# A graph layer's own rows: four transfers instead of one, sums of shares in PSUM, and a strip added in five parts

## The chip, the core and the metric

The kernel runs on one core of a Trainium2 chip. The metric is the device time of one execution in microseconds, taken as the median of several runs. The core has a matrix engine (TensorE: PE, with its weight loads as PEld), a vector engine (VectorE: DVE), a scalar engine (ScalarE: ACT), GpSimd (POOL) and an engine for synchronisation (SyncE: SP). Here POOL issues the gathers of rows and SP issues nearly all other transfers.

## The reference

One layer of a graph network over 50,000 nodes with 160 features and 1,650,000 edges, which are sorted by destination. 800,000 random pairs give an edge in each direction, and every node has an edge to itself.

```python
s, v = x[:, :64], x[:, 64:].reshape(n, 32, 3)
ss, vv = s[src], v[src]
e0, e1 = sh[:, 0:1], sh[:, 1:4]              # edge_attr_4
dot = einsum('eui,ei->eu', vv, e1)
out0 = C0 * (ss * e0 @ W1 + dot * INV3 @ W2)
p3 = (ss @ W3)[:, :, None] * e1[:, None, :] * INV3
p4 = einsum('eui,uw->ewi', vv * e0[:, :, None], W4) * INV3
p5 = einsum('eui,uw->ewi', cross(vv, e1[:, None, :]), W5) * INV6
m = concat([out0, (C1 * (p3 + p4 + p5)).reshape(-1, 96)])
m_agg = segment_sum(m, dst)
h = concat([m_agg[:, :64] @ Ws * LIN_S, (vector part of m_agg) @ Wv * LIN_V])
return layernorm(x + x + relu(h))
```

All of it up to the relu is linear in the source's row and in the edge's four attributes. So for every node it is enough to have four weighted sums of source rows, one for each attribute k: the sum over its edges of attr[e, k] * x[src[e]]. One product with a combined weight matrix then gives h.

## The kernel before

**Gathers and group sums.** Edges are taken in groups of 6 x 128, two groups to a "pair", 1044 pairs in all. For each pair POOL issues 12 indirect gathers, each of 128 rows of x, into a tile `xg` (line 349; four such tiles exist). DVE builds `hot` (line 358: which of a window of 32 nodes an edge belongs to; one input, `slotsP`, lies in PSUM) and `ha` (line 361: hot times the four attributes `pk`, which lie in PSUM). PE multiplies ha with the gathered rows (line 386), so that PSUM holds, for 4 attributes x 32 nodes, the sums over the group. DVE transposes them in blocks of 32 (line 398) and adds them at the right columns of a ring buffer (line 405, columns from a register).

**The ring.** `ring[k]` holds the sums of segment k, which is 512 nodes (S = 512), as 128 partitions (4 attributes x 32 features) x 5 blocks of features x TW = 768 nodes. Since sums of a segment's last groups run past its end, the first 256 columns of the next segment get what stands beyond column 512 of the one before (line 402, one addition over 5 x 256 columns, both inputs in SBUF).

**Own rows.** After the first 100 groups, edges that lead from a node to itself are no longer gathered. A "pack" step (16 packs, lines 463 to 628) takes them out of the edge lists: it compacts the other edges into `edges` in DRAM, sums each node's attributes of its own edges, and stores these "shares", four numbers a node, in `selves` in DRAM. Then for each two blocks of 128 nodes, `ask_own` (lines 661 to 684) loads their 256 rows of x into `xr`, once for each of the four attributes, which are four quarters of 32 partitions: partition 32k + w holds 8 nodes for attribute k. The load is one transfer whose source has a leading dimension of four copies with step 0 (line 675). A second transfer (line 676) loads into `sr` the one share that belongs to each partition and node. `set_own` (lines 686 to 696) multiplies xr by sr on DVE (line 689, both inputs in SBUF) and transposes the result into the ring (line 693), where later sums are added to it.

**Nodes.** For each block of 128 nodes PE multiplies the ring's five blocks with the weights (line 704), DVE adds x and takes mean and variance (lines 182 to 186), ACT takes the root (line 191), DVE scales (lines 195, 196), and SP stores two blocks at once (line 784). `ahead` loads x for this (line 644).

**Order.** The order is written by hand. `after_pair(p, f, ...)` hands f over when the program has written out pair p; `work(1.0)` then takes tasks from a queue, one credit for each gather's matmul. For a segment that begins at pair p (10 to 12 pairs after the one before), `begin_segment` is handed over at p - 3, ask_own at p - 6 and set_own at p - 2. Packs have due times (line 834), the earlier of one that follows from when the packed edges are loaded and one that follows from the first segment that needs their shares. Every engine runs its instructions in the order written; SP's queue holds the loads, the stores of packs (line 618) and the stores of results in one order.

**PSUM.** `bank` (line 243) is one bank of 4 x 128 numbers a partition. Its first quarter is `slotsP`; the second and third take transposes of indices (lines 326, 327); columns 0 to 19 of the fourth take the first node of each group (line 320).

Of the kernel before, what the change touches and what calls it, by code (L numbers as in the profile page):

```python
# [39 lines left out]
F32 = mybir.dt.float32  # L40
# [4 lines left out]
ALU = mybir.AluOpType  # L45
AX = mybir.AxisListType
# [4 lines left out]
P = 128  # L51
MUL0, MUL1 = 64, 32
D = MUL0 + 3 * MUL1
NK = 4
# [9 lines left out]
W = 32  # L64
QG = P // W
FB = P // NK
ND = D // FB
PG = 2
# [3 lines left out]
BP = 2  # L72
# [30 lines left out]
def tile_gnn_resnorm(ctx: ExitStack, tc: tile.TileContext, x, src, dst, attr, W1, W2, W3, W4, W5, Ws, Wv, out, n_edges):  # L103
    nc = tc.nc
# [97 lines left out]
    def near(g):  # L202
        p = g * G * P
        return p / degree if p <= EH else EH / degree + (p - EH) / (degree - 1)

    nblocks = math.ceil(N / P)
    S = SB * P
# [11 lines left out]
    high = [min(math.ceil(near(g)) + off_of[g // SG] + 1, N - 1) for g in range(NG)]  # L219
# [3 lines left out]
    TW = max(h - k * S for h, k in zip(high, seg_of)) + W  # L223
    first_of = [seg_of.index(k) for k in range(NSEG)]
    last_of = [max(g for g in range(NG) if low[g] < (b + 1) * P) for b in range(nblocks)]

    with tc.tile_pool(name="once", bufs=1) as once, tc.tile_pool(name="raw", bufs=2) as rawp, \
# [8 lines left out]
        spotp, ownp = (later_pools.enter_context(tc.tile_pool(name=name, bufs=bufs))  # L236
                       for name, bufs in (("spot", 3), ("own", 2)))
# [5 lines left out]
        bank = psC.tile([P, 4, P], F32, name="bank")  # L243
        slotsP = bank[:, 0, :]
        nc.vector.tensor_copy(slotsP, slots)

        dq = nc.sync
        begun = []
# [27 lines left out]
        spot_of, spots_of, ring = {}, {}, {}  # L276
# [117 lines left out]
        def turn_sums(p, ps):  # L394

            s, g, ng = pairs[p]
            at = sump.tile([P, PG, ND, W], F32, name="sums")
            nc.vector.transpose(at[:, :ng], ps[:, :ng].rearrange("p g (b f) -> p g b f", f=FB))  # L398
            for i in range(ng):
                k = seg_of[g + i]  # L400
                if k and g + i == first_of[k]:
                    nc.vector.tensor_tensor(ring[k][:, :, :TW - S], ring[k][:, :, :TW - S], ring[k - 1][:, :, S:],  # L402
                                            op=ALU.add)
                here = ring[k][:, :, ds(find(g + i), W)]
                nc.vector.tensor_tensor(here, here, at[:, i], op=ALU.add)  # L405

# [6 lines left out]
        def row_start(r):  # L413

            lo, hi = (math.floor(r * L * (1 - 1 / degree)) - 2 * FAR - 2, math.ceil(r * L * (1 - 1 / degree)) + 2 * FAR + 2)
            return (max(lo, 0), hi if r else 0), (max(math.floor((EH + r * L) / degree) - FAR - 2, 0),
                                                  math.ceil((EH + r * L) / degree) + FAR + 2)

        edges = dram.tile([1, (row_start(NR - 1)[0][1] + L) * C], F32, name="edges")
        selves = dram.tile([1, (row_start(NR - 1)[1][1] + W) * NK], F32, name="selves")  # L420
# [209 lines left out]
        def rows_of(b):  # L630
            nb = min(P, N - b * P)
            return nb, slice(b * P, b * P + nb)
# [25 lines left out]
                return []  # L658
            return [list(range(b, min(b + BP, nblocks))) for b in range(k * SB, min((k + 1) * SB, nblocks), BP)]

        def ask_own(k, bs, got):

            n0, n1 = rows_of(bs[0])[1].start, rows_of(bs[-1])[1].stop
            assert rows_stored[0] == NR or row_start(rows_stored[0])[1][0] >= n1
            n = n1 - n0
            nq = next(q for q in range(math.ceil(n / W), n + 1) if n % q == 0)
            m = n // nq
            assert nq <= BP * P // W
            xr = ownp.tile([P, BP * P // W, D], F32, name="xr")
            sr = ownp.tile([P, BP * P // W], F32, name="sr")  # L670
            xs = x[n0:n1, :].rearrange("(w q) d -> w (q d)", q=nq).unsqueeze(0).to_broadcast([NK, m, nq * D])
            ss = selves[0, n0 * NK:n1 * NK].rearrange("(w q k) -> k w q", q=nq, k=NK)
            with nc.allow_non_contiguous_dma(reason="one number of each node"):
                if m == W:
                    dq.dma_start(xr[:, :nq].rearrange("p q d -> p (q d)"), xs)
                    dq.dma_start(sr[:, :nq], ss)
                else:
                    nc.vector.memset(xr[:, :nq], 0.0)
                    nc.vector.memset(sr[:, :nq], 0.0)
                    for k_ in range(NK):  # L680
                        r = slice(k_ * W, k_ * W + m)
                        dq.dma_start(xr[r, :nq].rearrange("p q d -> p (q d)"), xs[k_])
                        dq.dma_start(sr[r, :nq], ss[k_])
            got.extend((xr, sr, nq))

        def set_own(k, bs, got):

            xr, sr, nq = got
            nc.vector.tensor_tensor(xr[:, :nq], xr[:, :nq], sr[:, :nq].unsqueeze(2).to_broadcast([P, nq, D]), op=ALU.mult)  # L689
            c0 = bs[0] * P - k * S  # L690
            c1 = (bs[-1] + 1) * P - k * S
            assert c0 + nq * W <= TW
            nc.vector.transpose(ring[k][:, :, c0:c0 + nq * W].rearrange("p b (w q) -> p q b w", q=nq),  # L693
                                xr[:, :nq].rearrange("p q (b f) -> p q b f", f=FB))
            if c0 + nq * W < c1:
                nc.vector.memset(ring[k][:, :, c0 + nq * W:c1], 0.0)
# [28 lines left out]
        spots = once.tile([1, 2 * npacks * RP], I32, name="spots")  # L725
        limit = once.tile([P, 1], F32, name="limit")
        nc.vector.memset(limit, float(KM))
        none = once.tile([P, 1], I32, name="none")
        nc.vector.memset(none, 0)
        packed = once.tile([P, 2, 2 * npacks], F32, name="packed")  # L730
# [10 lines left out]
        def after_pair(p, f, *args):  # L741
            later.setdefault(p, []).append((f, args))
# [83 lines left out]
        per = SG // PG  # L826

        packs, due = [], []
        for i in range(npacks):

            first = next(s for s in range(NH // SG, NSC)
                         if min(NG, (s + 1) * SG) * G * P - EH > row_start(i * RP)[0][0])
            own = next((k for k in range(NSEG) if min((k + 1) * S, N) > row_start(i * RP)[1][0] and own_blocks(k)), NSEG - 1)
            due.append(min((first - 1) * per - 1, first_of[own] // PG - 7))
            packs.append(pack(i))
        done, began = 0, START

# [1 line left out]
        for k in range(1, NSEG):  # L839
            p = first_of[k] // PG  # L840
            after_pair(max(p - 3, START), begin_segment, k)
            for bs in own_blocks(k):
                got = []
                after_pair(p - 6, ask_own, k, bs, got)
                after_pair(p - 2, set_own, k, bs, got)
        for b, g in enumerate(last_of):
            p = g // PG
# [5 lines left out]
        for p, (s, g, ng) in enumerate(pairs):  # L853
# [34 lines left out]
            if p == START - 1:  # L888
                with ExitStack() as behind, tc.tile_pool(name="table", bufs=1) as tablep:
                    for i in first_ones:  # L890
# [3 lines left out]
                               allow_small_or_imprecise_dtypes=True)  # L894
# [13 lines left out]
    base = const.tile([P, NB], F32, name="base")  # L908
# [6 lines left out]
    with tc.tile_pool(name="up", bufs=1) as up, tc.tile_pool(name="us", bufs=2) as us, tc.For_i(0, once_more, 1):  # L915
# [12 lines left out]
                       allow_small_or_imprecise_dtypes=True)  # L928
        nc.gpsimd.iota(hib, pattern=[[NBLK, CB]], base=NBLK, channel_multiplier=NBLK * CB,
                       allow_small_or_imprecise_dtypes=True)  # L930
        nseg = NU // SEG
        far = up.tile([PB, 2, CB, nseg], F32, name="far2")
        for s in range(nseg):
# [4 lines left out]
                           allow_small_or_imprecise_dtypes=True)  # L938
            nc.gpsimd.iota(num[:, 1], pattern=[[1, SEG]], base=s * SEG + 1, channel_multiplier=0,
                           allow_small_or_imprecise_dtypes=True)  # L940
# [10 lines left out]
        f = up.tile([PB, CB], F32, name="f")  # L951
# [104 lines left out]
```

## Time and profile before

| What | us |
|---|---|
| Median of 3 runs | 17993.09 (17978.58 to 18013.7) |
| Profiled execution, its own time | 18022.17 |
| Profiled execution, span | 18020.0 |
| Stream transpose of own rows, line 693, x188 | 466.1 busy, 2479 ns each |
| Group sums into PSUM, line 386, x25044 | 6255.4 busy on PE |
| Move of group sums, line 398, x1044 | 529.7 busy, 507 ns each; 6341.5 idle before them |
| Clearing of a ring, line 653, 128x1280, x93 | 104.6 busy, 1125 ns each |
| Granted TensorE clock, mean | 0.625 |

The profile is of one execution. "Busy" counts the time in which an engine executed, "idle before" the time that its engine stood before an instruction of the group, with what ended it; "issue" there is time in which the engine waited for nothing that the profile shows, and "remote" a release that the profile couldn't place. SPq marks issues on SP's queue. The mean of a group can hide a long tail, which the minimum, median and maximum of a line show. In 40 equal slices of the span every engine's share is nearly the same from start to end, so one stretch can stand for the others.

### The profile page before, as it was taken

The page shows a single profiled execution, that of the slowest core. Times are in us where ns is not written, and L with a number is a line of the kernel's source. Part 1 is how long each engine was busy: PE and PEld are TensorE (multiplying, and loading weights), DVE is VectorE, ACT ScalarE, POOL GpSimd, SP SyncE. Part 2 cuts the span into 40 slices and gives each one's busy share as a digit, 9 for nine tenths or more (in the row PEclk, how much of TensorE's full clock was granted, in tenths as well). Part 3 has the DMA queues.
Part 4 walks back from the last instruction along what each step waited for, and adds up shares of the span by engine and source line. Part 5 has one row for each costly group of instructions (what it writes and reads, how often), then busy time and mean ns, then how long its engine had stood idle before and what let it go on. Part 6 is the DMA issues. An engine that isn't in the chain of part 4 may idle for free. (4 is left out here: it accounts for less than half of the span.)

```text
span 18020.0 us, 99721 instructions
## 1 busy us (share of the span) xinstructions
PE 6879.0 (38%) x29811; PEld 6014.7 (33%) x29812; DVE 7032.6 (39%) x11269; ACT 227.8 (1%) x479; POOL 12137.8 (67%) x12535
## 2 busy tenths in 40 slices
PE   3333334343333333333333333334333333333333
PEld 3333333333333333333333333333333333333333
DVE  4343443434434343443433434344343433434332
ACT  0000000000000000000000000000000000000000
POOL 6666666666666666666666666666666666666666
PEclk6666666666666666666666666666666666666666
DMA  2222323232232322323223232322323223232222
GB/s 71 74 69 72 80 71 81 69 82 72 73 79 70 83 71 73 79 69 81 72 72 79 70 79 72 82 69 72 80 70 82 69 73 80 69 79 72 73 72 63
DMA packets 961715, 1337.18 MB, mean 74 GB/s; under 512 B 411739, under 2 KB 716048, under 8 KB 957182
## 3 DMA queue, kind: packets, MB, share of 16 engines
q0 software_dynamic: 601056, 1026.60, 23.7%
q1 hardware_dynamic: 358674, 302.87, 6.1%
q8 instruction: 238, 3.90, 0.1%
q14 instruction: 307, 2.51, 0.0%
q10 hardware_dynamic: 1440, 1.29, 0.0%
HBM read 1258.50 MB, written 71.40 MB: 74 GB/s over the span
## 5 line engine op out<-in xcount | busy, mean ns | idle before, releaser
L349 POOL DMA_INDIRECT xg<-in_x,si x12522 | 12134.1, 969 | 5859.5 <-issue 3666.1
L386 PE MATMUL ps<-xg,ha 128*128 128x160 f32 x25044 | 6255.4, 383 | 9081.8 <-issue 8146.9
L386 PEld LDWEIGHTS ps<-xg,ha 128*128 128x128 f32 x25044 | 5171.1, 254 | 9859.0 <-issue 8902.6
L398 DVE STREAM_TRANSPOSE sums<-ps 128x320 f32<-128x320 f32 x1044 | 529.7, 507 | 6341.5 <-remote 4050.5
L361 DVE TENSOR_TENSOR ha<-hot,pk 128x1536 f32<-128x1536 f32 x1044 | 1830.2, 1753 | 35.8
L182 DVE SCALAR_TENSOR_TENSOR y<-phb,xt 128x160 f32<-128x160 f32 x391 | 125.6, 321 | 3508.3 <-PE ps L386 1623.2
L704 PE MATMUL phb<-BWk,ring 128*128 128x160 f32 (+1 forms) x3910 | 1181.7, 388 | 454.0 <-issue 452.9
L704 PEld LDWEIGHTS phb<-BWk,ring 128*128 128x128 f32 (+1 forms) x3910 | 925.6, 266 | 470.0 <-issue 469.5
L405 DVE TENSOR_TENSOR ring<-ring,sums 128x160 f32 x2087 | 683.1, 327 | 309.7 <-issue 224.2
L358 DVE TENSOR_TENSOR hot<-bank,rel 128x384 f32<-128x384 f32 x1044 | 572.4, 548 | 107.0 <-remote 70.5
L693 DVE STREAM_TRANSPOSE ring<-xr 128x1280 f32<-128x1280 f32 x188 | 466.1, 2479 | 6.5
L566 DVE COPY_PREDICATED prow<-marks,prow 128x2370 f32<-128x2370 int32 (+8 forms) x160 | 445.4, 2784 | 1.1
L320 PE MATMUL bank<-first,ones 120*128 120x20 f32 (+1 forms) x210 | 59.4, 365 | 815.1 <-DVE first L318 573.0
L320 PEld LDWEIGHTS bank<-first,ones 120*128 120x128 f32 (+1 forms) x210 | 49.8, 292 | 853.6 <-DVE first L318 597.5
L191 ACT ACTIVATE rstd<-mv,eps_t 128x1 f32<-128x1 f32 x391 | 115.2, 295 | 17061.4 <-DVE st L184 5415.1
L326 PE MATMUL bank<-ident,r 120*128 120x120 f32 x100 | 46.2, 462 | 703.1 <-issue 361.0
L566 DVE COPY_PREDICATED pra<-marks,pra 128x1580 f32<-128x1580 int32 (+8 forms) x160 | 306.5, 1915 | 0.0
L689 DVE TENSOR_TENSOR xr<-xr,sr 128x1280 f32<-128x1280 f32 x188 | 277.0, 1473 | 57.4 <-DMA sr<-selves 35.9
L326 PEld LDWEIGHTS bank<-ident,r 120*128 120x128 f32 x100 | 21.1, 211 | 727.4 <-issue 369.7
L196 DVE TENSOR_SCALAR o<-y,mv,rstd 128x160 f32<-128x160 f32 x391 | 146.1, 374 | 19.6 <-issue 3.7
L402 DVE TENSOR_TENSOR ring<-ring 128x1280 f32<-128x1280 f32 x97 | 143.0, 1474 | 1.8
L331 PE MATMUL pk<-ident,r 120*128 120x120 f32 (+1 forms) x400 | 139.5, 400 | 0.0
(349 smaller groups left out, 2156.2 us busy)
## 6 DMA issues: line engine op xcount, KB each, us to landing
xg<-in_x,si POOLq DMA_INDIRECT x12522
xr<-in_x SPq DMA_DIRECT2D x187, 640.0 KB
edges<-prow SPq DMA_DIRECT2D x1994, 18.5 KB
r<-edges SPq DMA_DIRECT2D x99, 360.0 KB
selves<-mine SPq DMA_DIRECT2D x1992, 0.5 KB
xt<-in_x SPq DMA_DIRECT2D x195, 160.0 KB
out<-o SPq DMA_DIRECT2D x195, 160.0 KB
pra<-in_attr SPq DMA_DIRECT2D x15, 1580.0 KB
```

The costliest lines, as they stand in the source:

```text
L196: nc.vector.tensor_scalar(o[:n], y[:n], mv[:n, 0:1], rstd[:n], op0=ALU.subtract, op1=ALU.mult)
L349: nc.gpsimd.indirect_dma_start(out=xg[:, j, :], out_offset=None, in_=x, in_offset=bass.IndirectOffsetOnAxis(ap=placed[0][:, u + j:u + j + ...
L358: nc.vector.tensor_tensor(hot[:, :n], slotsP[:, 0:W].unsqueeze(1).to_broadcast([P, n, W]), rel[:, u:u + n].unsqueeze(2).to_broadcast([P, n ...
L361: nc.vector.tensor_tensor(ha[:, :n], hot[:, :n].unsqueeze(2).to_broadcast([P, n, NK, W]), pk[:, :, u:u + n].rearrange("p k u -> p u k").un ...
L386: mm = nc.tensor.matmul(ps[:, j // G, :], ha[:, j].rearrange("p k w -> p (k w)"), xr, start=j % G == 0, stop=j % G == G - 1)
L398: nc.vector.transpose(at[:, :ng], ps[:, :ng].rearrange("p g (b f) -> p g b f", f=FB))
L402: nc.vector.tensor_tensor(ring[k][:, :, :TW - S], ring[k][:, :, :TW - S], ring[k - 1][:, :, S:], op=ALU.add)
L405: nc.vector.tensor_tensor(here, here, at[:, i], op=ALU.add)
L566: nc.vector.copy_predicated(what[:n, a:e], mi[:, r].unsqueeze(2).to_broadcast([n, e - a, what.shape[2]]), what[:n, a + d:e + d])
L689: nc.vector.tensor_tensor(xr[:, :nq], xr[:, :nq], sr[:, :nq].unsqueeze(2).to_broadcast([P, nq, D]), op=ALU.mult)
L693: nc.vector.transpose(ring[k][:, :, c0:c0 + nq * W].rearrange("p b (w q) -> p q b w", q=nq), xr[:, :nq].rearrange("p q (b f) -> p q b f", ...
L704: wrote("misc", nc.tensor.matmul(ph[:nb], ring[k][:, i, c0:c0 + nb], BWk[:, i, :], start=i == 0, stop=i == ND - 1))
```

## The change

Four things change. The rows of x for own edges are loaded by four transfers of 32 partitions each, handed over at p - 8, p - 7, p - 6 and p - 5, in place of one of 128 partitions at p - 6. The shares are loaded as they lie in DRAM, all four of each node to every partition (`sa`, 8 nodes x 4 shares), together with the first part. set_own multiplies sa by a constant mask `shareP` (1 where the partition's quarter is k), sums over k into `sumP`, and multiplies xr by sumP; shareP and sumP lie in PSUM, in unused columns of `bank`. Last, the strip that passes from one ring to the next is added in five operations, one for each block of features, and only over `past` columns, as far as sums of the segment before can reach. The packs' due time by the segment's need is two pairs earlier, in step with the earlier first part.

```diff
+        shareP, sumP = bank[:, 3, 64:64 + NK], bank[:, 3, 96:96 + BP * P // W]
...
-                    nc.vector.tensor_tensor(ring[k][:, :, :TW - S], ring[k][:, :, :TW - S], ring[k - 1][:, :, S:],
-                                            op=ALU.add)
+                    past = max(high[first_of[k - 1]:first_of[k]]) + W - k * S
+                    for b in range(ND):
+                        nc.vector.tensor_tensor(ring[k][:, b, :past], ring[k][:, b, :past], ring[k - 1][:, b, S:S + past],
+                                                op=ALU.add)
...
-        def ask_own(k, bs, got):
+        def ask_own(k, bs, got, part):
...
-            xs = x[n0:n1, :].rearrange("(w q) d -> w (q d)", q=nq).unsqueeze(0).to_broadcast([NK, m, nq * D])
-            ss = selves[0, n0 * NK:n1 * NK].rearrange("(w q k) -> k w q", q=nq, k=NK)
...
-                    dq.dma_start(xr[:, :nq].rearrange("p q d -> p (q d)"), xs)
-                    dq.dma_start(sr[:, :nq], ss)
...
+            if part == 0:
+                xr = ownp.tile([P, BP * P // W, D], F32, name="xr")
+                sa = ownp.tile([P, BP * P // W, NK], F32, name="sa")
...
+            r = slice(part * W, part * W + m)
+            dq.dma_start(xr[r, :nq].rearrange("p q d -> p (q d)"), x[n0:n1, :].rearrange("(w q) d -> w (q d)", q=nq))
+            shares = selves[0, n0 * NK:n1 * NK].rearrange("(w f) -> w f", w=m)
+            if m < W:
+                dq.dma_start(sa[r, :nq].rearrange("p q k -> p (q k)"), shares)
+            elif part == 0:
+                dq.dma_start(sa[:, :nq].rearrange("p q k -> p (q k)"),
+                                shares.unsqueeze(0).to_broadcast([NK, W, nq * NK]))
...
-            nc.vector.tensor_tensor(xr[:, :nq], xr[:, :nq], sr[:, :nq].unsqueeze(2).to_broadcast([P, nq, D]), op=ALU.mult)
+            nc.vector.tensor_tensor(sa[:, :nq], sa[:, :nq], shareP.unsqueeze(1).to_broadcast([P, nq, NK]), op=ALU.mult)
+            nc.vector.tensor_reduce(sumP[:, :nq], sa[:, :nq], axis=AX.X, op=ALU.add)
+            nc.vector.tensor_tensor(xr[:, :nq], xr[:, :nq], sumP[:, :nq].unsqueeze(2).to_broadcast([P, nq, D]), op=ALU.mult)
...
+        quarter = once.tile([P, NK], F32, name="quarter")
+        of_k = once.tile([P, NK], F32, name="of_k")
+        nc.gpsimd.iota(quarter, pattern=[[-W, NK]], base=0, channel_multiplier=1, allow_small_or_imprecise_dtypes=True)
+        nc.vector.tensor_scalar(of_k, quarter, 0.0, None, op0=ALU.is_ge)
+        nc.vector.scalar_tensor_tensor(shareP, quarter, float(W), of_k, op0=ALU.is_lt, op1=ALU.mult)
...
-            due.append(min((first - 1) * per - 1, first_of[own] // PG - 7))
+            due.append(min((first - 1) * per - 1, first_of[own] // PG - 9))
...
-                after_pair(p - 6, ask_own, k, bs, got)
+                for part in range(NK):
+                    after_pair(p - 8 + part, ask_own, k, bs, got, part)
```

## The prediction

> **What bounds the kernel now.** I read the engine sums and the costliest groups first, then POOL's waits, then timelines and a table by stretch. The groups (line, engine, operation, tile; busy us, mean ns of one; idle time before them and what ended it):
>
> ```profile
> PE 6879.0 (38%) x29811; PEld 6014.7 (33%) x29812; DVE 7032.6 (39%) x11269; ACT 227.8 (1%) x479; POOL 12137.8 (67%) x12535
> ...
> L349 POOL DMA_INDIRECT xg<-in_x,si x12522 | 12134.1, 969 | 5859.5 <-issue 3666.1
> ...
> L361 DVE TENSOR_TENSOR ha<-hot,pk 128x1536 f32<-128x1536 f32 x1044 | 1830.2, 1753 | 35.8
> ...
> L405 DVE TENSOR_TENSOR ring<-ring,sums 128x160 f32 x2087 | 683.1, 327 | 309.7 <-issue 224.2
> ...
> L689 DVE TENSOR_TENSOR xr<-xr,sr 128x1280 f32<-128x1280 f32 x188 | 277.0, 1473 | 57.4 <-DMA sr<-selves 35.9
> ...
> L402 DVE TENSOR_TENSOR ring<-ring 128x1280 f32<-128x1280 f32 x97 | 143.0, 1474 | 1.8
> ```
>
> POOL does nothing but 12,522 gathers. The answer on line 349 gives their median as 949 ns. POOL's waits (total us, times, longest):
>
> ```profile
> POOL xg L349 <- issue: 3666.1, 11991, 2.1
> POOL xg L349 <- PE ps L386: 1224.7, 236, 46.9
> POOL xg L349 <- remote: 875.2, 223, 7.0
> ```
>
> Between gathers that wait for nothing lie 3666.1/11991 = 0.306 us. So the span divides: 12,522 x (0.949 + 0.306) = 15,715 us of floor; 12,134.1 - 12,522 x 0.949 = 251 us by which gathers are longer than the median; and pauses of 1224.7 + 875.2 + some 93 in smaller rows = 2193, of which 531 x 0.306 = 162 is floor already, leaving 2031. With 30 us before the first and after the last gather that is 18,027 against a span of 18,020.
>
> The pauses come about like this (timeline; start, us, engine, line; in brackets idle time before):
>
> ```profile
> 2999.47 0.42 PE L704 MATMUL phb<-BWk,ring 128*128 128x160 f32 x1 [2.38 <-issue]
> ...
> 3002.27 0.43 PE L386 MATMUL ps<-xg,ha 128*128 128x160 f32 x1 [2.38 <-issue]
> ...
> 3005.77 6.51 PE L386 MATMUL ps<-xg,ha 128*128 128x160 f32 x32
> ...
> 3006.24 0.95 POOL L349 DMA_INDIRECT xg<-in_x,si  x1 [6.21 <-PE phb L704]
> ```
>
> While POOL gathers without a break, PE slows to one instruction in 0.70 or 1.40 us, though its rows have long been there; the four tiles of xg fill, POOL stands 6.21 us, and PE at once runs 32 matmuls in 6.51 us. SP shows the same 0.70 us steps. These pauses return every 24 or 36 gathers from start to end. So POOL is the bound, but with a tax on every gather.
>
> **What the long gathers cost.** Here two of them stand beside the product:
>
> ```profile
> 1415.84 0.95 POOL L349 DMA_INDIRECT xg<-in_x,si  x1 [0.30 <-issue]
> 1415.89 1.48 DVE L689 TENSOR_TENSOR xr<-xr,sr 128x1280 f32<-128x1280 f32 x1
> ...
> 1417.09 1.09 POOL L349 DMA_INDIRECT xg<-in_x,si  x1 [0.31 <-issue]
> ...
> 1419.74 2.32 POOL L349 DMA_INDIRECT xg<-in_x,si  x1 [0.30 <-issue]
> 1419.76 1.48 DVE L689 TENSOR_TENSOR xr<-xr,sr 128x1280 f32<-128x1280 f32 x1
> ```
>
> The gather that starts with the second product takes 2.32 us. I laid all gathers of the timeline beside the DVE lines they overlap and summed what they took over 949 ns (counting those over 970): beside L689, 186 gathers and 184 us; beside L402, 96 gathers and 51 us, part of which belongs to the L405 right behind it. Beside L361, whose second input is in PSUM, it is 6 us over 2196 gathers. L689 and L402 read both inputs from SBUF.
>
> Do these microseconds count? The stretches (length, POOL busy and its gathers, granted clock, DMA):
>
> ```profile
> 146.00:745.00 599.00, 400.40 (x420) 0.62 0.25 64
> 3191.00:3790.00 599.00, 405.98 (x421) 0.62 0.29 71
> 14633.00:15231.00 598.00, 409.97 (x421) 0.63 0.32 80
> ```
>
> The first lies before the first L689 (840.7 us). The later ones carry 5.6 and 9.6 us more POOL time for the same gathers and take no longer: pauses shrink as the gathers stretch. To put a number on it I cut the gather stream into pieces of 48, left out those with a pause over 7 us, and fitted length against the excess in it: 0.23 (+-0.14) us per us. Pieces of 24 to 180 gave 0.16 to 0.51. I take 0.3; ends 0 and 1.
>
> **The change, part by part.**
>
> *Product from PSUM.* sumP takes the place of sr, so the product has L361's operands: one in SBUF, one in PSUM. L361 costs 1753 ns for 1536 elements and L358 548 for 384, 1.046 ns an element, so 1280 take 1.49 us against 1.473: nothing on DVE. The 184 us of excess go. Times 0.3: -55 us (0 to -184).
>
> *Two small operations before it.* Nearest rows: L358 scaled to 32 elements, 548 - 352 x 1.046 = 180 ns, and the reduction at L341 (278 ns for 120 elements), some 190 ns. 188 x 0.37 = 70 us of DVE, none with two SBUF inputs. The three set-up operations cost under 1 us, once.
>
> *Strip in five parts.* `past` from the plan's numbers is 133 to 256 columns, mean 215 (256 before). Between L405 (160: 327 ns) and L402 (1280: 1474) lies 1.024 ns an element, so a piece is 383 ns and five are 1.91 us against 1.47: 97 x 0.44 = +43 us of DVE. L405 is the row for a piece: outside L402's surroundings it lengthens gathers by some 29 us over 2087, 14 ns each, so 485 pieces give 7 us against 51. Times 0.3: -13 us (0 to -44; +0 if a piece blocks like a fifth of the whole).
>
> These +113 us of DVE I cost at nothing: DVE is busy 39%, and its group sums<-ps idles 6341.5 us waiting for PE. With no cover at all they are +113. What a late set_own holds up is hot and ha (L358, L361) queued behind it on DVE, then PE.
>
> *Four transfers, one of shares.* SP's queue (issues, with the time SP was held):
>
> ```profile
> 1232.34 0.57 SPq L675 DMA_DIRECT2D xr<-in_x  x1
> ...
> 1233.54 12.48 SPq L675 DMA_DIRECT2D xr<-in_x  x1
> ```
>
> Two issues per pair of blocks become five: 187 x 3 = 561 more, at L676's median 0.53 us, 297 us of SP; at the 1.40 of the slow spells 785. Removed are spells like the 12.48, one in each of 93 segments if parts no longer fill the queue: up to 93 x 11.9 = 1107 us. SP waits 4767.2 us for DVE's o at L784, which covers either. Costed 0; ends below. The first part is asked at p-8 and needs the buffer that set_own of the segment before (10 to 12 pairs earlier, at p-2) frees: free by then, and the sends queued behind it wait for later DVE work. Only the first pack's due time moves (38 to 36; the others are set by the edges' term).
>
> The Trainium skill speaks against four transfers: "DMA: Bandwidth & Descriptors", Rules for kernel authors, says two transfers to disjoint partition parts serialize and one over 128 partitions is better. The same table says that an outermost dimension of four copies keeps a transfer to four engines, which is how xr is asked today and fits the 12.48 us hold. By the first rule the loads would last longer, by the second shorter; neither moves the sum while the loads come early.
>
> They do: from the issue of sr to its product pass 99 us or more in three quarters of the cases.
>
> *Sum.* -55 - 13 = -68 on 18,020: 17,952. The profiled run's 18,022 stands 29 us above the median of three, 17,993.09, so -68 there gives **17,925 us**. I count under 0.2% (36 us) as no change.
>
> **Rivals.**
> *B, every microsecond counts* (pass-through 1): -228, 17,765. For: POOL is the bound. Against: the three stretches.
> *C, all absorbed, or the product still blocks*: 17,990. For: the first stretch has hardly any excess and is no faster; PE's slow spells set the rhythm. Against: fits of 0.16 to 0.51, none at 0; L361's 6 us.
> *D, slower: the fourth part lands late at pack ends.* It is asked at p-5, one pair (18,020/1044 = 17.3 us) later than xr today. Where SP is busy storing a pack, sr is issued only 12 to 55 us before the product (24 of 187 cases, some 12 pack ends). With 17 us less, DVE would stand there, ha behind it, PE behind that. The cover is the rows waiting in xg; beyond it POOL pauses. At about 10 us for each of 12 to 16 pack ends it is +120 to +160: 18,130 us. It decides where the lead today is under 17 us plus landing. Against: the 12.5 us hold that eats that lead goes; DVE has waited for sr just 53.6 us in all, 7 times. The extra DVE work without cover (+113) ends at the same place.
>
> **How the numbers follow.** A (partial) 0.52, B 0.12, C 0.16, D 0.20. A's own range is 17,875 to 17,960 by pass-throughs 0.51 to 0.16; 0.06 of it lies within 0.2%. Faster: 0.46 + 0.12 = 0.58; same: 0.06 + 0.16 = 0.22; slower: 0.20. The range cuts off about half of B and half of D: 17,800 to 18,080.
>
> **What would show it.** After: mean gather near 951 ns (POOL busy some 11,910); no long gather beside the product; L402's successor with 485 pieces near 383 ns; the product near 1.48 us; SP's holds on x gone. If pauses (PE ps + remote, 2100 us) rise by 160 or so, A holds; if they stay, B; by 228, C. A wait of DVE on xr or sa in the hundreds of us, or POOL pauses over 10 us at more pack ends than today, shows D. I am wrong if the pauses change for a reason of their own: they are 2031 us, nine times what is removed, and a tenth of them outweighs the sum.

## The result, and the profile after

Twenty runs of each kernel on one chip: 17,992.66 us before, 18,020.46 us after (17,999.86 to 18,037.71), ratio 1.0015, 95% interval 1.0008 to 1.0022. The change lost 0.15%, inside the 0.2% that I count as no change, where 0.4% was to be gained. The profiled execution's span is 18,025.6 us, against 18,020.0.

The groups of the changed kernel (line, engine, operation, tile; busy us, mean ns of one; idle time before them), with the engine sums ahead:

```profile
PE 7001.9 (39%) x29811; PEld 6106.9 (34%) x29812; DVE 7105.0 (39%) x12035; ACT 228.4 (1%) x479; POOL 11879.9 (66%) x12536
...
L350 POOL DMA_INDIRECT xg<-in_x,si x12522 | 11876.1, 948 | 6114.2 <-issue 3647.6
...
L694 DVE TENSOR_TENSOR xr<-xr,bank 128x1280 f32<-128x1280 f32 x188 | 278.8, 1483 | 61.7 <-DMA xr<-in_x 53.8
...
L405 DVE TENSOR_TENSOR ring<-ring 128x196 f32<-128x196 f32 (+20 forms) x485 | 149.0, 372 | 1.8
```

POOL's busy time fell from 12,137.8 to 11,879.9 us, by 258 us, and a gather's mean from 969 to 948 ns. That is all the prediction wanted from the gathers. The product takes 1483 ns and a piece of the strip 372. Two products in the timeline, with the gathers beside them:

```profile
2715.15 0.95 POOL L350 DMA_INDIRECT xg<-in_x,si  x1 [0.30 <-issue]
...
2715.63 1.49 DVE L694 TENSOR_TENSOR xr<-xr,bank 128x1280 f32<-128x1280 f32 x1
...
2716.41 0.95 POOL L350 DMA_INDIRECT xg<-in_x,si  x1 [0.32 <-issue]
...
2719.93 1.49 DVE L694 TENSOR_TENSOR xr<-xr,bank 128x1280 f32<-128x1280 f32 x1
2720.16 0.95 POOL L350 DMA_INDIRECT xg<-in_x,si  x1 [0.30 <-issue]
```

No gather is stretched here: the three that overlap a product take 0.95 us, where one took 2.32 before. Over all 188 products the gathers beside them are longer by 0.2 us in total, where it was 184. But the span did not shrink, and POOL's waits say where the time went (us in total, times, longest):

```profile
POOL xg L350 <- issue: 3647.6, 11959, 1.1
POOL xg L350 <- PE ps L387: 1449.7, 251, 35.3
POOL xg L350 <- remote: 901.4, 226, 6.8
```

The waits for PE and the unplaced ones went from 1224.7 + 875.2 = 2099.9 to 1449.7 + 901.4 = 2351.1 us, up 251. The gathers gave 258 us and POOL's pauses took 251. The three stretches that the prediction looked at (length, POOL busy and its gathers, granted clock, DMA share, GB/s) agree:

```profile
146.00:745.00 599.00, 380.39 (x402) 0.63 0.23 62
3191.00:3790.00 599.00, 392.80 (x415) 0.62 0.27 70
14633.00:15231.00 598.00, 391.88 (x415) 0.62 0.30 80
```

Per gather the later two have fallen from 964 and 974 ns to 947 and 944, 7 to 12 us for 420 gathers, yet 415 fit into the stretch in place of 421. The first stretch lies ahead of the first product, and has 402 for 420 by pauses of its own.

From here on I split what a trace shows of POOL in one manner for all kernels. "Long" is the sum of what the gathers longer than 949 ns took over that; "pauses" the sum of the idle stretches over 0.6 us ahead of a gather, less 0.305 us each. Before, they are 264 and 2034 us; after, 39 and 2293. So 225 of the 258 us were long gathers. The other 33 us come from a median gather of 946 ns in place of 949; the changed kernel's second trace has 949 again, so they are not due to the change.

### The profile page after: what moved, and what is told of

Same layout as the page of the kernel before. It is cut to its first block, busy times and chain, and to the rows that moved or that the text cites. A ratio compares the mean times of both kernels' runs of the same rounds, so it can differ in the third digit from the quotient of the medians.

```text
span 18025.6 us, 101276 instructions
## 1 busy us (share of the span) xinstructions
PE 7001.9 (39%) x29811; PEld 6106.9 (34%) x29812; DVE 7105.0 (39%) x12035; ACT 228.4 (1%) x479; POOL 11879.9 (66%) x12536
## 5 line engine op out<-in xcount | busy, mean ns | idle before, releaser
L350 POOL DMA_INDIRECT xg<-in_x,si x12522 | 11876.1, 948 | 6114.2 <-issue 3647.6
L387 PE MATMUL ps<-xg,ha 128*128 128x160 f32 x25044 | 6387.7, 388 | 8839.7 <-issue 8130.5
L387 PEld LDWEIGHTS ps<-xg,ha 128*128 128x128 f32 x25044 | 5278.0, 258 | 9628.9 <-issue 8903.5
L694 DVE TENSOR_TENSOR xr<-xr,bank 128x1280 f32<-128x1280 f32 x188 | 278.8, 1483 | 61.7 <-DMA xr<-in_x 53.8
L405 DVE TENSOR_TENSOR ring<-ring 128x196 f32<-128x196 f32 (+20 forms) x485 | 149.0, 372 | 1.8
L184 DVE BATCH_NORM_STATS2 st<-y 128x6 f32<-128x160 f32 x391 | 128.1, 328 | 13.4
```

Source lines behind the costliest of these rows:

```text
L350: nc.gpsimd.indirect_dma_start(out=xg[:, j, :], out_offset=None, in_=x, in_offset=bass.IndirectOffsetOnAxis(ap=placed[0][:, u + j:u + j + ...
L387: mm = nc.tensor.matmul(ps[:, j // G, :], ha[:, j].rearrange("p k w -> p (k w)"), xr, start=j % G == 0, stop=j % G == G - 1)
L405: nc.vector.tensor_tensor(ring[k][:, b, :past], ring[k][:, b, :past], ring[k - 1][:, b, S:S + past], op=ALU.add)
L694: nc.vector.tensor_tensor(xr[:, :nq], xr[:, :nq], sumP[:, :nq].unsqueeze(2).to_broadcast([P, nq, D]), op=ALU.mult)
```

## The experiments

### The parts by themselves

Four kernels on one chip, where the kernel before took 18,111.33 us (33 runs). The first has nothing of the change but the product's second input in PSUM, through a copy:

```diff
+            nc.vector.tensor_copy(sumP[:, :nq], sr[:, :nq])
-            nc.vector.tensor_tensor(xr[:, :nq], xr[:, :nq], sr[:, :nq].unsqueeze(2)...
+            nc.vector.tensor_tensor(xr[:, :nq], xr[:, :nq], sumP[:, :nq].unsqueeze(2)...
```

> The kernel before with one edit: sr is copied to PSUM and the product reads it there; loads, times of asking and the strip stay. Theory T (POOL's pauses answer for whatever the gathers save, so microseconds inside gathers count for nothing): POOL busy falls by some 180 us, POOL's pauses rise by as much, the time stays within 0.1% of before. Rival R1 (the saved microseconds count, and another part of the change gives them back): the time falls by 0.3 to 1.0%, 60 to 180 us.

The second has the strip in five parts alone:

```diff
-                    nc.vector.tensor_tensor(ring[k][:, :, :TW - S], ring[k][:, :, :TW - S], ring[k - 1][:, :, S:], op=ALU.add)
+                    past = max(high[first_of[k - 1]:first_of[k]]) + W - k * S
+                    for b in range(ND):
+                        nc.vector.tensor_tensor(ring[k][:, b, :past], ring[k][:, b, :past], ring[k - 1][:, b, S:S + past], op=ALU.add)
```

> The kernel before with the strip in five parts alone. T: POOL busy falls by some 40 us, the time stays within 0.1%. R1: it falls by up to 0.2%. Rival R2 (more DVE instructions are what costs): it rises by up to 0.25% (43 us of DVE).

The third has the four transfers and the earlier due time, with sr loaded as before beside the first:

```diff
-                after_pair(p - 6, ask_own, k, bs, got)
+                for part in range(NK):
+                    after_pair(p - 8 + part, ask_own, k, bs, got, part)
```

> The kernel before with the four transfers of x at p-8 to p-5 and the packs' due time two pairs earlier; sr, product and strip as before. T with the loss in the first pack: +0.1 to +0.2% (some 25 us), all of it in the first 850 us. R3 (561 more issues on SP cost everywhere): a rise spread over the whole span. R1 would put the whole loss of the change here: more than +0.5%.

The fourth has the due time alone:

```diff
-            due.append(min((first - 1) * per - 1, first_of[own] // PG - 7))
+            due.append(min((first - 1) * per - 1, first_of[own] // PG - 9))
```

> The kernel before with the due time of the packs alone two pairs earlier, which by the plan's numbers moves only the first pack (38 to 36). If the long pauses of the changed kernel near 703 and 837 us come from this, the time rises by 0.1 to 0.2% (25 us) here too; if they come from the transfers, it stays within 0.05%.

| Kernel | median us | ratio (95%) | long | pauses |
|---|---|---|---|---|
| product from PSUM | 18,141.47 | 1.0019 (1.0010 to 1.0029) | 90 | 2326 |
| strip in five | 18,110.18 | 0.9999 (0.9990 to 1.0008) | 208 | 2226 |
| four transfers | 18,087.83 | 0.9985 (0.9976 to 0.9994) | 266 | 2101 |
| due time | 18,111.42 | 1.0000 (0.9991 to 1.0009) | 269 | 2119 |

The product from PSUM takes 179 us out of the gathers (269 to 90, against the last row), and POOL's pauses grow by 207: no gain, but a loss of 30 us, more than the 0.1% that theory T allowed. The copy to PSUM, 36.5 us of DVE in all, is in this kernel alone, and its part in the loss isn't known. The strip takes out 61 and pauses grow by 107, with no difference in time. The four transfers are the only part that gains, 24 us, with the gathers as long as before; none of the expectations had that. The due time alone moves nothing, but whether the gain comes from the division into four or from the times of asking was not separated. In that kernel SP is held over 5 us by an issue on x 8 times, against 93 in the trace of before. The three ratios multiply to 1.0003, where the full change gave 1.0008 (0.9998 to 1.0017) and 1.0015 in its two measurements, so no large cost lies outside these parts.

### Runs without pauses

Kernels that were run together on one chip, one after the other, are called a session here. The session of the next four met something that I had not expected: the kernel before itself took 16,008.90 us there (9 runs). The first is the changed kernel with all four parts of x asked for at p - 6 and the due time of before:

```diff
-                    after_pair(p - 8 + part, ask_own, k, bs, got, part)
+                    after_pair(p - 6, ask_own, k, bs, got, part)
-            due.append(min((first - 1) * per - 1, first_of[own] // PG - 9))
+            due.append(min((first - 1) * per - 1, first_of[own] // PG - 7))
```

> The changed kernel with all four transfers asked at p-6, as xr was before, and the packs' old due time. T2 (the loss comes from the product that no longer stretches gathers, not from when loads are asked): as the changed kernel, ratio to before 1.001 to 1.002. Rival (timing of the loads): back to 1.000 or below.

The second is the changed kernel with the sums in SBUF, so that both of the product's inputs lie there again:

```diff
+            sr = ownp.tile([P, BP * P // W], F32, name="sr")
-            nc.vector.tensor_reduce(sumP[:, :nq], sa[:, :nq], axis=AX.X, op=ALU.add)
+            nc.vector.tensor_reduce(sr[:, :nq], sa[:, :nq], axis=AX.X, op=ALU.add)
-            nc.vector.tensor_tensor(xr[:, :nq], xr[:, :nq], sumP[:, :nq].unsqueeze(2)...
+            nc.vector.tensor_tensor(xr[:, :nq], xr[:, :nq], sr[:, :nq].unsqueeze(2)...
```

> The changed kernel with the sums of shares in SBUF in place of PSUM, so that the product again has both inputs in SBUF; all else stays. T2 (a gather stretched by 1 us at this place spares at least as much pause later): POOL's long gathers rise by some 180 us, its pauses fall by 200 or more, ratio to before 0.998 to 1.000, so faster than the changed kernel. T (long gathers and pauses exchange one for one): 1.0015. R1 (long gathers count): 1.011.

The first took 15,751.54 us, 0.9840 of the kernel before (0.9827 to 0.9853); the second 15,886.08, 0.9925 (0.9911 to 0.9939). The groups and POOL's waits of the first:

```profile
L350 POOL DMA_INDIRECT xg<-in_x,si x12522 | 11899.5, 950 | 3829.3 <-issue 3530.7
...
L694 DVE TENSOR_TENSOR xr<-xr,bank 128x1280 f32<-128x1280 f32 x188 | 278.8, 1483 | 7.4 <-DVE bank L693 1.1
```

```profile
POOL xg L350 <- issue: 3530.7, 11576, 1.0
POOL xg L350 <- PE ps L387: 230.5, 756, 0.3
```

The mean gather is 950 ns, as in the changed kernel above, but POOL's longest wait for PE is 0.3 us: there are no pauses (8 us in all). Its timeline shows PE beside the gathers:

```profile
2994.41 0.95 POOL L350 DMA_INDIRECT xg<-in_x,si  x1 [0.30 <-issue]
...
2994.53 0.90 PE L387 MATMUL ps<-xg,ha 128*128 128x160 f32 x2 [0.44 <-DMA xg<-in_x,si]
2995.67 0.95 POOL L350 DMA_INDIRECT xg<-in_x,si  x1 [0.30 <-issue]
...
2995.73 0.90 PE L387 MATMUL ps<-xg,ha 128*128 128x160 f32 x2 [0.29 <-DMA xg<-in_x,si]
```

PE keeps step: it makes two matmuls for each gather and then waits for the next rows to land, 1.25 us from one gather to the next. None of the 0.70 us steps are there. The same groups of the second kernel:

```profile
L350 POOL DMA_INDIRECT xg<-in_x,si x12522 | 12029.7, 961 | 3828.3 <-issue 3543.2
...
L695 DVE TENSOR_TENSOR xr<-xr,sr 128x1280 f32<-128x1280 f32 x188 | 280.2, 1490 | 8.2 <-DVE sr L694 1.8
```

The product's duration is the same; the gathers carry 12,029.7 - 11,899.5 = 130 us more, and the kernel takes 134.5 us more. On this chip, at that time, every microsecond that the product adds to gathers counts. None of the expectations had such a session in view, but by the difference of the two kernels, 0.85%, R1 is right there.

The other two added work to POOL behind the gathers of the changed kernel, to see what spread-out rests do. One writes 64 numbers after each gather, the other 790 after the last of each pair (`if j == n - 1`):

```diff
+                if True:
+                    nc.gpsimd.iota(idle, pattern=[[1, 64]], ...)
```

> The changed kernel with a small iota on POOL (64 numbers a partition into an unused tile) after every gather, some 0.18 us each by the iota rows (138 ns for 20, 231 for 128), 2230 us in all. If POOL's pauses only make room for engines that its unbroken gathers slow down, these small breaks take the place of the 2300 us of pauses: PE's spells of 0.70 and 1.40 us steps shrink, and the time changes by -1 to +3%. If the pauses have a cause of their own (PE too slow, buffers too few), POOL's work and the pauses add: +10 to +12%.

> The changed kernel with one iota of 790 numbers on POOL after each pair's gathers (792 ns by its row), 1044 x 0.79 = 825 us in all. One for one with the pauses: within 0.5%. If a break of 0.8 us is too short to let the other engines catch up, it adds: up to +4.6%.

They took 18,921.31 us (1.1820, 1.1802 to 1.1838) and 16,649.56 us (1.0401, 1.0385 to 1.0417). Both answered another question than mine: with no pauses there was nothing to replace, and as nothing tied these writes to their gathers they were moved together into clumps (one of 625 us in the second). They show that POOL's work adds in full there: 0.25 us for each of 12,522 (18,921.31 - 15,751.54 = 3170 us), 0.86 us for each of 1044, both against the kernel with all parts at p - 6, since the changed kernel unaltered was not run there.

### The changed kernel, rests, products and SBUF sums where there are pauses

The kernel before took 18,159.79 us here (25 runs). The changed kernel, unaltered:

> The changed kernel once more, beside the others of this batch. Theory 1 (two regimes): on a chip where the kernel before takes some 18,000 us the pauses of POOL above 0.6 us sum to over 2,000 us and the ratio is 1.000 to 1.003; on a chip where the kernel before takes some 16,000 us there are hardly any pauses and the ratio is 0.982 to 0.986 (all that the long gathers lose). Theory 2 (the chip plays no part, the time at which the four parts of x are asked does): the ratio is 1.000 to 1.003 on either chip.

The changed kernel with 800 numbers written by POOL into each xg tile ahead of its gathers, so that the write can't move:

```diff
             xg = rowp.tile([P, PG * G, D], F32, name="xg")
+            nc.gpsimd.iota(xg[:, 0:5, :].rearrange("p j d -> p (j d)"), pattern=[[1, 5 * D]], ...)
```

> The changed kernel, and POOL writes 800 numbers into each xg tile ahead of its first gather, some 0.81 us by 0.797 us for 790 numbers in the run before, 1044 times, 845 us in all and spread evenly. Theory 1: on a chip with pauses the added 845 us take the place of pauses, and the time stays within 150 us of the changed kernel's; on a chip without pauses POOL is at its floor and all 845 us are added. Theory 2 (POOL is the bound on either chip and its pauses are a property of what it waits for): 700 to 900 us are added on either.

The changed kernel with the first product of each group made twice:

```diff
             for j, xr in enumerate(rows):
+                if j % G == 0:
+                    wrote("ps", nc.tensor.matmul(ps[:, j // G, :], ha[:, j].rearrange("p k w -> p (k w)"), xr, start=True, stop=True))
```

> The changed kernel, and the first product of each group is made twice: 2087 more weight loads and 2087 more matmuls on PE. Theory 1: on a chip with pauses PE's instruction rate (0.70 us an instruction while POOL gathers without a break) sets the time; slow steps of PE fill some 6640 of 18,026 us, so 2087 x 1.40 us x 6640/18026 = 1076 us is the upper estimate, and at least 300 us are added; on a chip without pauses PE is some 2.6 us behind the gathers with room to spare, and under 30 us are added. Theory 2 (POOL is the bound in both): under 60 us on either.

And the kernel with the sums in SBUF once more:

> The changed kernel with the summed shares in SBUF, so that both inputs of the product lie there. Theory 1: on a chip with pauses POOL's gathers grow by 130 to 180 us and its pauses shrink by about as much, and the time is within 0.2% of the changed kernel's, or up to 0.2% faster; on a chip without pauses it is 130 to 150 us slower than the changed kernel. Theory 2 (gathers count in full on either chip): 130 to 180 us slower on either.

| Kernel | median us | ratio (95%) | long | pauses |
|---|---|---|---|---|
| changed | 18,172.23 | 1.0008 (0.9998 to 1.0017) | 41 | 2399 |
| with rests | 18,366.51 | 1.0109 (1.0092 to 1.0126) | 67 | 2629, of which 845 are the writes |
| more products | 18,202.44 | 1.0025 (1.0015 to 1.0034) | 38 | 2457 |
| sums in SBUF | 18,166.70 | 1.0001 (0.9991 to 1.0011) | 159 | 2282 |

The last row against the first is the cleanest test of the prediction's factor. The gathers' rows of the two, changed first and sums in SBUF second, and the waits in the same order:

```profile
L350 POOL DMA_INDIRECT xg<-in_x,si x12522 | 11911.7, 951 | 6221.9 <-issue 3645.0
```

```profile
L350 POOL DMA_INDIRECT xg<-in_x,si x12522 | 12028.9, 961 | 6105.5 <-issue 3644.8
```

```profile
POOL xg L350 <- PE ps L387: 1449.3, 246, 37.3
POOL xg L350 <- remote: 993.0, 224, 7.1
```

```profile
POOL xg L350 <- PE ps L387: 1440.6, 245, 35.1
POOL xg L350 <- remote: 929.7, 245, 6.8
```

117 us more in gathers, 117 us less in pauses, and 5.5 us less in time: what added 134.5 us in the session without pauses adds nothing here.

The rests cost 194 us of their 845, between the 150 of theory 1 and the 700 of theory 2:

```profile
L349 POOL IOTA xg<- 128x800 f32 x1044 | 844.7, 809 | 1923.4 <-PE ps L389 1047.4
```

POOL's other pauses fell from 2399 to 2629 - 845 = 1784 us, by 615. So a rest at the head of every tile replaces pauses for most of its own length. The added products (two matmuls and two weight loads on PE for each call, so 4174 of each and not the 2087 of the expectation) cost 30 us:

```profile
L390 PE MATMUL ps<-xg,ha 128*128 128x160 f32 x25044 | 6296.1, 376 | 5143.8 <-issue 4928.8
...
L388 PE MATMUL ps<-xg,ha 128*128 128x160 f32 x4174 | 1316.8, 395 | 3113.6 <-issue 2896.6
```

1316.8 us of further matmuls moved the time by 30 us, where theory 1 asked for at least 300. Nor did they lengthen the idle time of PE that has no cause in the profile, 4928.8 + 2896.6 = 7825 us before these products. In the changed kernel it is:

```profile
PE ps L387 <- issue: 8114.3, 3789, 58.6
```

That PE's rate of instructions as such sets the time is refuted.

### How far POOL may run ahead

Two kernels changed the tiles that gathers fill. The first has eight tiles of 6 gathers in place of four of 12:

```diff
-            xg = rowp.tile([P, PG * G, D], F32, name="xg")
+            rows = []
             for j in range(n):
+                if j % G == 0:
+                    xg = rowp.tile([P, G, D], F32, name="xg")
+                rows.append(xg[:, j % G, :])
...
-tc.tile_pool(name="rows", bufs=4)
+tc.tile_pool(name="rows", bufs=8)
```

> The changed kernel with xg in eight tiles of 6 gathers in place of four of 12, the same bytes. On a chip with pauses (kernel before some 18,000 us) nearly every pause stands ahead of the first gather of a tile (439 of 444 after the first 600 gathers in the profile of the changed kernel) and waits until PE has used up a whole tile. Theory A (a pause is one tile's worth of PE's work, and there are as many): their sum, 2293 us, falls towards half, and the time by 500 to 1100 us. Theory B (PE is late by an amount of its own, and pauses only hand it on): their sum stays within 150 us, and the ratio to the kernel before between 0.997 and 1.005. On a chip without pauses both expect what the changed kernel has there, 0.982 to 0.987.

The second has two tiles of 12 (bufs=2):

> The changed kernel with two xg tiles of 12 gathers in place of four. On a chip with pauses, theory A expects as many pauses or more of the same 4 to 6 us, 18,000 to 18,600 us. Theory B expects that POOL is let run ahead of PE by 24 gathers less (30 us by 1.25 us), so that each lateness of PE above that becomes a pause: over 1.03 of the kernel before. On a chip without pauses, where PE is 2.6 us behind the gathers, both expect under 1.00.

With them went the kernel with all parts asked for at p - 6:

> The changed kernel with its four parts of x asked for together six pairs ahead. Theory 1 (what the long gathers lose comes back as pauses on a chip that has them): ratio 0.998 to 1.003 where the kernel before takes some 18,000 us, 0.984 where it takes some 16,000 us. Theory 2 (asking at six pairs is what made the run of 0.984): 0.984 to 0.990 on either.

This was again a session without pauses (before 15,973.49 us), and all three took the same: 15,718.63, 15,719.10 and 15,715.23 us, ratios 0.9841, 0.9841 and 0.9839, each with an interval of 0.0032 to 0.0033 in width. The first two ask at p - 8 to p - 5 like the change, so neither the tiles nor the time of asking matters there, and the gain of 1.6% is not due to asking at p - 6. Whether that time of asking gains where there are pauses wasn't seen. The two with tiles ran once more, with the kernel before itself for its profile:

> The kernel with eight xg tiles of 6 gathers again, since the run before had no pauses to tell the theories apart. On a chip with pauses: theory A (a pause is one tile's worth of PE's work, as many of them) 500 to 1100 us less than the changed kernel's 18,020 to 18,170 us; theory B (PE is late by an amount of its own) ratio 0.997 to 1.005. Without pauses: 0.984, as before.

> The kernel with two xg tiles of 12 gathers again. On a chip with pauses: theory A 18,000 to 18,600 us; theory B over 1.03 of the kernel before, since POOL may run ahead of PE by 24 gathers (30 us) less. Without pauses: 0.984, as before.

> The kernel before itself, for its profile on this chip. Both theories: ratio 1.000. Without pauses, theory 1 expects some 260 us of long gathers and under 20 us of pauses, so that the 258 us between this kernel and the changed one lie in the gathers alone; with pauses, some 2,000 us of them.

Now there were pauses (before 18,126.38 us, 19 runs):

| Kernel | median us | ratio (95%) | long | pauses, number |
|---|---|---|---|---|
| eight tiles of 6 | 17,982.85 | 0.9916 (0.9899 to 0.9932) | 36 | 2260, 563 |
| two tiles of 12 | 18,126.24 | 0.9997 (0.9987 to 1.0006) | 38 | 2405, 483 |
| before | 18,129.44 | 0.9997 (0.9987 to 1.0008) | 267 | 2185, 444 |

The two lower rows are the exchange again: 229 us out of the gathers, 220 into the pauses, 3 us in time. And the middle row says that running ahead by 24 gathers less costs nothing that shows: it stands at 0.9997 of the kernel before, where the changed kernel with four tiles stood at 1.0008. Its timeline through one pause:

```profile
9041.41 0.90 PE L387 MATMUL ps<-xg,ha 128*128 128x160 f32 x2 [0.25 <-DMA xg<-in_x,si]
...
9042.78 0.51 PE L387 MATMUL ps<-xg,ha 128*128 128x160 f32 x1 [0.47 <-DMA xg<-in_x,si]
...
9045.58 0.42 PE L387 MATMUL ps<-xg,ha 128*128 128x160 f32 x1 [2.29 <-issue]
...
9048.39 0.42 PE L387 MATMUL ps<-xg,ha 128*128 128x160 f32 x1 [2.39 <-issue]
...
9051.18 0.42 PE L387 MATMUL ps<-xg,ha 128*128 128x160 f32 x1 [2.36 <-issue]
9051.35 0.95 POOL L350 DMA_INDIRECT xg<-in_x,si  x1 [0.30 <-issue]
...
9053.98 0.42 PE L387 MATMUL ps<-xg,ha 128*128 128x160 f32 x1 [2.38 <-issue]
...
9056.09 5.39 PE L387 MATMUL ps<-xg,ha 128*128 128x160 f32 x14 [0.28 <-issue]
...
9058.76 0.95 POOL L350 DMA_INDIRECT xg<-in_x,si  x1 [6.46 <-PE ps L387]
```

Until 9042 us PE is in step with the gathers. Then the matmuls come 2.8 us apart, each after 2.3 to 2.4 us of idle time for which the profile shows no cause, while POOL gathers on to the end of its tiles at 9051. Some 4 us after POOL's last gather has ended PE is quick again (14 matmuls in 5.39 us), and POOL, released, starts a gather at 9058.76. So here a pause comes with a slow spell, and a longer way ahead doesn't avoid it: with four tiles POOL is only stopped later in the spell. When a pause begins, POOL is some 30 gathers ahead of PE with four tiles (the changed kernel above), some 6 with two (medians). PE's idle time without a cause shows the same, four tiles first (the kernel before, run beside it), two tiles second:

```profile
PE ps L386 <- issue: 8068.9, 3676, 71.8
```

```profile
PE ps L387 <- issue: 3534.9, 2601, 27.1
```

PE's slow time is less than half with two tiles, yet the pauses are as many as in the changed kernel with four (483 against 475) and sum to as much (2405 against 2399 us). So the pauses don't follow from how long PE is slow. POOL's waits, eight tiles first, two tiles second:

```profile
POOL xg L353 <- issue: 3586.4, 11688, 4.3
POOL xg L353 <- remote: 1364.0, 365, 6.5
POOL xg L353 <- PE ps L390: 1064.3, 355, 29.2
```

```profile
POOL xg L350 <- issue: 3636.6, 11910, 1.9
POOL xg L350 <- PE ps L387: 1562.9, 335, 34.1
POOL xg L350 <- remote: 888.5, 186, 6.9
```

With smaller tiles POOL resumes after a smaller piece of PE's work. The pauses are shorter, 2260/563 = 4.0 us for 2405/483 = 5.0, but there are more of them; the net is 145 us, and the time falls by 143. Neither theory had the size: A wanted 500 us at least, since it held the number of pauses for fixed; B wanted no gain here, and over 3% of loss with two tiles.

So the change with eight tiles of 6 gathers beats both kernels where there are pauses: 0.84% under the kernel before (0.68 to 1.01), and 143 us under the change with two tiles, which takes as long as the kernel before. Without pauses it is 1.59% under the kernel before (1.43 to 1.75), as are the other versions of the change; there the tiles add nothing. The changed kernel unaltered was not run in such a session.

## Why the prediction was wrong

Its steps on the parts held. The long gathers went, nearly to the microsecond that it summed (228 forecast; 225 by the same sum over 949 ns, 264 - 39). The product takes 1483 ns (1.49 us forecast), a piece of the strip 372 (383), the two small operations 175 and 195 (370 together, as forecast). The strip's further work on DVE cost nothing (18,110.18 against 18,111.33 us); that of the two small operations was not run alone. SP's holds on x over 5 us went from 93 to 1, and the time of SP on them from 1298 to 410 us in spite of four times the issues.

The step that failed is "Times 0.3", the share of the gathers' microseconds that passes through to the time. It was fitted from pieces of one trace, with the pieces that hold a pause over 7 us left out, and read as a property of the kernel. Between kernels it was -0.05 for the SBUF sums against the changed kernel (-5.5 us for +118), about 0 for two tiles against before, and -0.17 for the product alone (+30 us for 179 fewer). So where it put -55 us, the product alone measured +30, and where it put -13, the strip alone measured -1. The pauses rose by 251 us; the prediction had named a rise by 228 as the sign of rival C. The prediction's stretches showed this, as the argument for rival C said: the stretch without long gathers was no faster. I gave them less weight than a fit whose error was over half its value. That a fit inside one trace misses pauses that move to another piece is my explanation of its 0.23, and no run tests it.

Rival C (all absorbed, 17,990) is what happened, with 28 us more in the first session. Those 28 us I can't place: the profiled spans differ by 5.6 us, and the changed kernel's second measurement is 1.0008 with 1 inside its interval. The pauses of the first stretch don't settle it: the 541st gather starts at 837 us against 822 before, but in the later sessions with pauses at 820 to 840 in kernels that have the whole change and at 828 in the one before. Rival D is refuted: the four transfers alone gain 0.15%, and DVE waits 53.8 us for xr, on 3 occasions, as long as it waited for sr. POOL's pauses over 10 us, the other sign of D, are 19 after and 11 before, but 9 with the four transfers alone. By "DMA: Bandwidth & Descriptors", Rules for kernel authors, in the Trainium skill, two transfers to disjoint partition halves serialize, and one over 128 partitions is better; here the four, asked from two pairs earlier to one pair later, measured better than the one with an outermost dimension of four copies.

Rival B (every microsecond counts), which got 0.12, is right in the sessions without pauses: 257 us between the kernel before and the changed one with all parts at p - 6, for 233 us of long gathers (264 in the first profile of before, 31 in this kernel's). The kernel before has no trace of such a session, so the 24 us between the two can't be placed. The rule behind the part that works is in "SBUF — State Buffer", Who interferes with whom, of the same skill: a DVE instruction with two SBUF inputs contends with a GpSimd instruction that reads SBUF; one with at most one SBUF input, outside the modes that use two ports, doesn't. The traces agree (12,029.7 against 11,899.5 us of gathers with and without), and the gathers read their indices `si` from SBUF. The same section infers that such an operation would not hold up the making of descriptors. The runs don't settle that: they show that the gather as a whole took up to 2.32 us beside such a product, not which part of it waited.

What the pauses are was read only in part. The prediction called POOL the bound "with a tax on every gather". In the last two sessions with pauses the sum of long gathers and pauses stays within 2440 to 2452 us for the changed kernel, the one with SBUF sums, two tiles and before, while its parts shift by 230. It isn't a constant: it is 2298 before and 2332 after in the first session, 2367 to 2434 in the second, 2495 with more products and 2296 with eight tiles. Time that POOL spends stretched, writing or standing still is largely interchangeable where there are pauses, as if PE and SP needed it off the gathers; that fits these runs and is not proved by them. Gathering without a break does not by itself slow PE, as the prediction's reading had it: without pauses POOL does so from start to end, and PE keeps step. What sets the 0.70 us steps off, and what makes a session of one kind or the other, stays open. How far POOL may run ahead sets how long PE is slow, but not what the pauses sum to; PE's further matmuls and the due time hardly move them.

## What to carry to other kernels

The microseconds of an engine that has to pause at regular intervals need not count one by one, even if it is the busiest: compare stretches that have the cost with those that have not, and believe them over a fit. Before a small gain is put down to a change, time the kernel before beside it in more than one session, since this one has two rhythms: versions of the change are worth 1.6% in one, and the change is worth nothing in the other. Where an engine stands waiting for a whole tile to be used up, smaller tiles of the same total are a cheap thing to try; here they gained 0.8% in one session with pauses and nothing without.

## What the runs showed of the hardware that was not expected

The same kernel took 17,993, 18,111, 18,160 and 18,126 us in four sessions and 16,009 and 15,973 us in two others, with nothing between. It isn't a property of a numbered chip: the one with 16,009 us bears the same number as that with 18,126. Nor is it PE's clock, which is lower where the kernel is faster (0.57 against 0.62 for the kernel before). In the traces with pauses SP's register moves take 29 ns in the median and 690 ns at the upper quartile; in those without, 29 ns up to the 95th percentile.
